# Layer-norm transposes on 64 rows of the array, in two PSUM banks an image, and set-up products in the projection's banks

## The chip, the cores and the metric

The kernel runs on one core of one Trainium2 chip. The metric is the device time of one execution in microseconds; a lower number is better. The core has TensorE (PE, with its weight loads shown apart as PEld), VectorE (DVE), ScalarE (ACT), GpSimd (POOL) and SyncE (SP), 16 DMA engines shared by the queues, and PSUM, which holds what PE writes[...].

## The reference

`x` is float32, 16 images of 192 channels by 64 x 64 pixels. Two layers follow each other. Only the first lines concern the change:

```
h = layernorm over the 192 channels of each pixel (x)
projected, gate = split(h @ in_proj_w.T + b)        # 192 -> 2 x 192 channels
projected = depthwise3x3(projected)
scanned = mix of four directional scans of projected; local = depthwise3x3(projected)
mixed = (scanned + local) * sigmoid(gate)
mixed = gelu(batchnorm over images and pixels (mixed))
x = x + out_proj(mixed)
x = x + fc2(gelu(fc1(layernorm(x))))
# second layer
taps = small network of the mean of x over pixels      # per image and channel
out = masked depthwise3x3(x, taps) + bias
```

## The kernel before

Three stages run one after the other. The first (to about 628 us) does the layer norm and the input projection of all images and stores the result to HBM. The second (to about 1300 us) does the depthwise convolutions, scans, gate and the sums of the batch norm, by groups of 8 channels. The third does the rest by chunks of 512 pixels of an image pair. The change touches only the first.

The instructions of the five engines run in the order in which the program text issues them; semaphores that the framework derives from tiles hold them apart. A tile pool gives a tag so many buffers; a new tile of a tag waits until the readers and writers of the tile that had the buffer are done.

The first stage has 64 steps n (`n_ac`). A step holds 512 pixels of two images: `xa` is [128, 3, 512], where partitions 0 to 63 hold 64 channels of the first image, partitions 64 to 127 those of the second, and the middle index t runs over the three classes of 64 channels. `HALF` names the two partition halves, and `pixels(n, t, g)` is one class of one group g of 128 pixels; a step has AR = 4 groups. Four steps make a block (16 image rows of a pair).

For each step:

- `load_a(n + 3)` issues six loads of 128 KB (L473), three on SP's queue and three on POOL's. `xa` has four buffers, so a load waits until the projection of step n - 1 is done.
- `store_first` (L532) and `store` (L538) issue the stores of the block before, part by part (`PARTS` cuts the channel groups into 1, 7, 7, 5 and 3), on the SP and POOL queues.
- `turn(n + 1)` transposes the next step's pixels on PE into `ps_xt` (L485), so that each pixel has its channels along the free axis: 12 transposes of 128 x 128, for 3 classes and 4 groups. `ps_xt` has one buffer of three banks.
- `project(n)` (L514) multiplies, for each group, the raw pixels by the projection's weights, which already hold the layer norm's scale and have their column means taken away. For each of three classes there are two products, one for each image on its 64 rows of the array, [64 x 128 pixels] by [64 x 384], summed over the classes in PSUM tiles `ps_pj0` and `ps_pj1` of two buffers each. FP32 products appear as two records in the profile, transposes as one.
- `variance(n + 1, g)` on DVE takes the statistics of the next step's group g for both images (`bn_stats` L492, `bn_aggr` L493), issued ahead of the evacuation of group g.
- The evacuation multiplies the projection by 1/deviation and writes it to a staging tile: DVE takes `ps_pj0` (L519), ACT takes `ps_pj1` (L520). Blocks alternate between the staging tiles `stg` and `mid`, so the first evacuation of a block waits for the stores of the block before the last.
- `deviation(n + 1)` takes the square root on ACT (L497) and the reciprocal on DVE (L498).
- `side` adds set-up work to some steps: `diagonals`, `gate_bias`, `decay_rows`, `projection_bias`, `tap_sums`, `columns`, `sums_across`, `conv_bias`, `runs` and others. Those with a product on PE (steps 5 to 8 and 18 to 23, and two before the loop) take a PSUM bank from `bank()`, tag `pb` with one buffer (L268).

PSUM is filled before and after: before, `pb` has one bank, `xt` three and the `pj` tiles four.

The order of PE in step n is: turn(n + 1), projection of groups 0 to 3 of step n, set-up products of step n.

Of the kernel before, what the change touches and what calls it, by code (L numbers as in the profile page):

```python
# [21 lines left out]
F32 = mybir.dt.float32  # L22
# [5 lines left out]
C = 192  # L28
# [3 lines left out]
CH = 512  # L32
# [12 lines left out]
AR = CR // 2  # L45
# [10 lines left out]
def conv_block_kernel(ctx: ExitStack, tc: tile.TileContext, x, prm, w_in, w_out, w_fc1, b_fc1, w_fc2, w1, bn1, w2, out):  # L56
    nc = tc.nc
# [5 lines left out]
    HALF = (slice(0, 64), slice(64, 128))  # L63
# [26 lines left out]
    ident = cp.tile([128, 128], F32, tag="ident", name="ident")  # L90
# [159 lines left out]
    with ExitStack() as stage:  # L250
# [15 lines left out]
        ind = ka.tile([128, 3], F32, tag="ind", name="ind")  # L266

        def bank():  # L268
            return psa.tile([128, CH], F32, tag="pb", name="pb")

        def projection_weights():

            by_group = lambda v: v.rearrange("p (k g c) -> p g k c", k=2, c=GC)
            flat = lambda v: v.rearrange("p g k c -> p (g k c)")
            for t in range(3):
                nc.vector.tensor_scalar_mul(wi[:, t], by_group(w0[:, t]), pt3[:, t, LN1W:LN1W + 1])
            yield
            pc = bank()
            for t in range(3):
                nc.tensor.matmul(pc[:, 0:2 * C], mean_w, flat(wi[lo, t]), start=(t == 0), stop=(t == 2))  # L280
            yield
            for t in range(3):
                nc.vector.tensor_sub(flat(wi[:, t]), flat(wi[:, t]), pc[:, 0:2 * C])
            yield
# [11 lines left out]
        def gate_bias():  # L296
            pb = bank()
            for t in range(3):
                nc.tensor.matmul(pb[:, 0:C], lnb[:, t], w0[lo, t, C:2 * C], start=(t == 0), stop=False)
            for t in range(3):  # L300
                nc.tensor.matmul(pb[:, 64 * t:64 * t + 64], ones[lo], dg[:, t, 0], start=False, stop=(t == 2))
            nc.vector.tensor_copy(bias_g, pb[:, 0:C])
# [7 lines left out]
        def decay_rows():  # L310
            pd = bank()[:, 0:2 * C].rearrange("p (k c) -> p k c", k=2)
            for t in range(3):
                for k in range(2):
                    nc.tensor.matmul(pd[:, k, 64 * t:64 * t + 64], ones[lo], dg[:, t, 1 + k],
                                     start=(t == 0 and k == 0), stop=(t == 2 and k == 1))
            for k in range(2):
                by_half(dec_b[:, k], pd[:, k])
# [140 lines left out]
        psa = stage.enter_context(tc.tile_pool(name="psa", bufs=1, space=PSUM))  # L458
# [18 lines left out]
        def pixels(n, t, g):  # L477
            return ast[n]["xa"][:, t, g * 128:(g + 1) * 128]

        def turn(n):  # L480

            xt = psa.tile([128, 3, AR, 128], F32, tag="xt", name="ps_xt")
            for t in range(3):
                for g in range(AR):
                    nc.tensor.transpose(xt[:, t, g], pixels(n, t, g), ident)  # L485
            ast[n].update(xt=xt, st6=sp.tile([128, AR, 2, 6], F32, tag="st6", name="st6"),
                          mv=sp.tile([128, AR, 2, 2], F32, tag="mva", name="mva"))

        def variance(n, g):
            s = ast[n]  # L490
            for i, q in enumerate(HALF):
                nc.vector.bn_stats(s["st6"][:, g, i], s["xt"][:, :, g, q])  # L492
                nc.vector.bn_aggr(s["mv"][:, g, i], s["st6"][:, g, i])  # L493

        def deviation(n):
# [5 lines left out]
        def project(n, groups, beside_it):  # L501

            blk, part = divmod(n, per)
            if blk not in stag:
                if blk % 2:
                    both_i = mid.rearrange("p (i o j) -> p i o j", i=2, j=BR)
                else:
                    both_i = stg.tile([128, 2, 2 * C, BR], F32, tag="stg", name="stg")
                stag[blk] = [both_i[:, i] for i in range(2)]
            for g in groups:  # L510
                ps = [psa.tile([128, 2 * C], F32, tag=f"pj{i}", name=f"ps_pj{i}", bufs=2) for i in range(2)]
                for t in range(3):
                    for i, q in enumerate(HALF):
                        nc.tensor.matmul(ps[i], pixels(n, t, g)[q], wi[q, t].rearrange("p g k c -> p (g k c)"),  # L514
                                         start=(t == 0), stop=(t == 2))
                for v in beside_it(g) if n + 1 < n_ac else ():
                    variance(n + 1, v)
                j, rs = part * AR + g, ast[n]["rs"]
                nc.vector.tensor_scalar_mul(stag[blk][0][:, :, j], ps[0], rs[:, g, 0:1])  # L519
                nc.scalar.activation(stag[blk][1][:, :, j], ps[1], AF.Copy, scale=rs[:, g, 1:2])  # L520
# [44 lines left out]
        next(steps)  # L565
        next(steps)
        turn(0)
        for g in range(AR):
            variance(0, g)
        deviation(0)  # L570

        for n in range(n_ac):
            if n + 3 < n_ac:
                load_a(n + 3)
            blk, part = divmod(n, per)
            if blk:
                if part == 0:
                    store_first(blk - 1)
                    store(blk - 1, 0, (nc.gpsimd, nc.sync))
                store(blk - 1, part + 1, (nc.gpsimd, nc.sync))  # L580
                if part == per - 1:
                    stag.pop(blk - 1)

            h = AR // 2 if n == 0 else 0
            project(n, range(h), lambda g: ())
            if n + 1 < n_ac:
                turn(n + 1)
            project(n, range(h, AR), lambda g: (g,) if h == 0 else (2 * (g - h), 2 * (g - h) + 1))
            if n + 1 < n_ac:
                deviation(n + 1)  # L590
            for f, args in side.pop(n, ()):
                f(*args)
# [5 lines left out]
    with ExitStack() as stage:  # L598
# [168 lines left out]
        for k in range(-2, n_bp + 1):  # L767
            if 0 <= k + 1 < n_bp:
                tables(k + 1)
            if k >= 1:  # L770
                vertical(k - 1)
                gate(k - 1)
                g, c = divmod(k, hp_)
# [645 lines left out]
```

## Time and profile before

| | |
|---|---|
| median of 3 runs | 3594.07 us (3593.32 to 3596.56) |
| profiled execution | 3596.65 us, span 3594.9 us |
| busy share of the span | PE 99%, PEld 52%, DVE 76%, ACT 51%, POOL 32% |
| first stage, last projection record | 628.0 us |
| `ps_pj` L514, PE | 516.1 us, 3072 records, 488 ns mean |
| `ps_xt` L485, PE | 768 records, 273 ns median |
| `st` L492, DVE | 173.1 us, 512 times, 338 ns mean |
| granted clock of PE | 0.997 of full speed |

A record's length includes its latency, and records overlap: what an engine can do per microsecond is read from the distance between starts, not from the mean length. The DMA share is the mean busy share of the 16 engines; packets of two queues overlap in it, so it can pass 1.

### The profile page before, as it was taken

What the parts mean: (1) busy time and instruction counts of PE and PEld (TensorE: products, weight loads), DVE (VectorE), ACT (ScalarE), POOL (GpSimd) and SP (SyncE); (2) the same over time, 40 slices, a digit from 0 to 9 for tenths busy, and PEclk for the clock granted to TensorE, in tenths of its full rate; (3) what the DMA queues carried; (4) which work ended last, traced back from release to release, by engine and by line L of the source; (5) the groups of instructions that cost most, each with busy time, mean ns of one, the idle gap of its engine ahead of it and who ended that gap; (6) DMA issues with size and microseconds to landing.
All of it is one profiled execution on the core that took longest, in us unless ns stands there. A gap on an engine that the chain in (4) does not pass through costs nothing.

```text
span 3594.9 us, 77663 instructions
## 1 busy us (share of the span) xinstructions
PE 3572.8 (99%) x32658; PEld 1885.2 (52%) x32658; DVE 2748.3 (76%) x4722; ACT 1836.6 (51%) x2067; POOL 1156.2 (32%) x1246
## 2 busy tenths in 40 slices
PE   9999999999999999999999999999999999999998
PEld 6666666555566654445444444445444444444443
DVE  6878777899999985556777777677777767777765
ACT  3443334888888863434444453444445444444533
POOL 3434332111111123433333343433333343333433
PEclk9999999999999999999999999999999999999999
DMA  7898998999999961112222222222222222222213
GB/s 165 240 257 254 258 271 242 301 301 283 281 283 286 281 143 41 45 44 72 60 68 75 65 74 61 79 60 68 73 66 74 61 79 60 69 75 65 74 34 89
DMA packets 288981, 492.19 MB, mean 137 GB/s; under 512 B 24816, under 2 KB 183016, under 8 KB 288632
## 3 DMA queue, kind: packets, MB, share of 16 engines
q1 hardware_dynamic: 246772, 341.85, 35.5%
q0 software_dynamic: 40928, 144.36, 14.1%
q8 instruction: 257, 4.21, 0.5%
q10 hardware_dynamic: 932, 1.03, 0.1%
q14 instruction: 92, 0.75, 0.1%
HBM read 284.95 MB, written 197.92 MB: 134 GB/s over the span
## 4 chain that ended last, share of the span: by engine, by line
PE 90%; DVE 1%; DMA 1%; issue 0%; ACT 0%; ACTq 0%; SPq 0%; POOL 0%; DVEq 0%
PE ps_f L996 28%; PE ps_f L851 18%; PE ps_l L673 11%; PE ps_pj L514 8%; PE ps_d L629 7%; PE ps_s L851 7%; PE ps_o L906 5%; PE ps_o L899 2%; PE ps_xt L485 1%; PE ps_m L935 1%; PE ps_v L935 1%; PE ps_k L851 0%; DMA xa<-in_x_dram 0%; DVE o L65 0%; PE pb_h L141 0%
## 5 line engine op out<-in xcount | busy, mean ns | idle before, releaser
L996 PE MATMUL ps_f<-h,wf 64*64 64x512 f32 x9216 | 1015.0, 591 | 0.0
L998 ACT ACTIVATE gl<-ps_f,bf 128x1024 f32<-128x1024 f32 x384 | 427.9, 1114 | 1082.0 <-PE ps_f L996 1079.7
L996 PEld LDWEIGHTS ps_f<-h,wf 64*64 64x64 f32 x9216 | 346.9, 133 | 598.4 <-issue 574.6
L851 PE MATMUL ps_f<-gl,place 128*64 128x256 f32 (+1 forms) x3072 | 528.7, 486 | 1.1 <-ACT rs L978 1.1
L514 PE MATMUL ps_pj<-wi,xa 64*128 64x384 f32 x3072 | 516.1, 488 | 1.6 <-DVE mid L519 1.0
L514 PEld LDWEIGHTS ps_pj<-wi,xa 64*128 64x128 f32 x3072 | 292.8, 188 | 196.4 <-issue 11.6
L1031 POOL TENSOR_TENSOR gl<-gl 128x512 f32<-128x512 f32 x192 | 308.8, 1635 | 159.1 <-PE ps_f L851 159.1
L851 PEld LDWEIGHTS ps_f<-gl,place 128*64 128x64 f32 x3072 | 225.5, 137 | 217.4 <-issue 145.7
L1021 POOL COPY turn<-o 128x1 f32<-128x1 f32 x84 | 16.4, 195 | 832.8 <-DVE o L65 832.8
L1027 POOL TENSOR_TENSOR t<-gl 128x512 f32<-128x512 f32 x192 | 246.1, 1282 | 89.1 <-ACT gl L998 44.7
L1029 POOL TENSOR_TENSOR t<-gl,t 128x512 f32<-128x512 f32 x192 | 247.1, 1287 | 44.2 <-ACT gl L998 30.7
L473 POOL DMA_DIRECT2D xa<-in_x_dram x192 | 120.4, 635 | 362.5 <-PE ps_pj L514 319.8
L65 DVE SCALAR_TENSOR_TENSOR o<-ximg,taps,o 128x1024 f32<-128x1024 f32 x180 | 231.7, 1288 | 4.9
L664 DVE TENSOR_TENSOR_SCAN v<-tab,q 128x1024 f32<-128x1024 f32 x96 | 218.3, 2274 | 7.8 <-ACT tab L652 7.8
L666 DVE TENSOR_TENSOR_SCAN v<-tab,q 128x1024 f32<-128x1024 f32 x96 | 217.5, 2266 | 0.0
L520 ACT ACTIVATE mid<-ps_pj,rsa 128x384 f32<-128x384 f32 x128 | 120.3, 941 | 184.9 <-PE ps_pj L514 178.6
L520 ACT ACTIVATE stg<-ps_pj,rsa 128x384 f32<-128x384 f32 x128 | 120.3, 941 | 180.6 <-PE ps_pj L514 176.3
L1054 DVE SCALAR_TENSOR_TENSOR ximg<-ps_f,pt,ximg 128x256 f32<-128x256 f32 (+1 forms) x176 | 96.6, 549 | 151.2 <-PE ps_f L851 151.2
L652 ACT ACTIVATE tab<-mask,dec_b 128x1024 f32<-128x1024 f32 x192 | 209.8, 1146 | 0.0
L492 DVE BATCH_NORM_STATS2 st<-ps_xt 128x6 f32<-128x192 f32 x512 | 173.1, 338 | 15.6 <-PE ps_xt L485 14.8
L912 DVE SCALAR_TENSOR_TENSOR ximg<-ps_o,pt,low 128x256 f32<-128x256 f32 x264 | 113.1, 479 | 92.9 <-PE ps_o L906 90.2
L906 PE MATMUL ps_o<-low,wo 128*64 128x256 f32 x1536 | 182.1, 385 | 0.4 <-ACT low L879 0.4
(258 smaller groups left out, 5686.0 us busy)
## 6 DMA issues: line engine op xcount, KB each, us to landing
low<-in_x_dram SPq DMA_DIRECT2D x128, 384.0 KB
out_dram<-o SPq DMA_DIRECT2D x172, 256.0 KB
mid<-pg_d SPq DMA_DIRECT2D x8, 4096.0 KB
low<-mixed_d SPq DMA_DIRECT2D x116, 256.0 KB
low<-pg_d SPq DMA_DIRECT2D x7, 4096.0 KB
pg_o<-pg_d SPq DMA_DIRECT2D x7, 4096.0 KB
xa<-in_x_dram POOLq DMA_DIRECT2D x192, 128.0 KB, 5.6
xa<-in_x_dram SPq DMA_DIRECT2D x192, 128.0 KB
```

What stands on the lines that cost most here:

```text
L65: nc.vector.scalar_tensor_tensor(o, in0, scalar, in1, ALU.mult, ALU.add, **kw)
L514: nc.tensor.matmul(ps[i], pixels(n, t, g)[q], wi[q, t].rearrange("p g k c -> p (g k c)"), start=(t == 0), stop=(t == 2))
L520: nc.scalar.activation(stag[blk][1][:, :, j], ps[1], AF.Copy, scale=rs[:, g, 1:2])
L629: nc.tensor.matmul(dst(ps[o, ih]), mats[g % 2]["dm"][q, di + 1, :, ch], src(s["pg"][q, :, 0, ch]), start=(di == 0), stop=stop)
L673: nc.tensor.matmul(dst(bst[k]["ps"][o, i]), lm_of(g)[q, m, :, c], src(q, ih), start=start, stop=stop)
L851: nc.tensor.matmul(ps[q], w(i), rhs(i), start=start, stop=stop, **kw)
L906: nc.tensor.matmul(ps[wh][q].rearrange("p (r w) -> p r w", w=32), wo[:, 64 * t:64 * t + 64], cols(rows(s["mx"][:, i]))[:, :, wh], start=fi ...
L996: nc.tensor.matmul(pf[o, i], wf1[q, t, m0:m0 + 64], s["h"][q, t], start=(t == 0), stop=(t == 2))
L998: nc.scalar.activation(gl, pf, AF.Gelu, bias=bf1[:, m:m + 1])
L1027: sub(t1[:, m], b12(m), b11(m))
L1029: sub(t2[:, m], b22(m), t1[:, m])
L1031: sub(b12(m), b22(m), b12(m))
```

## The change

`turn` splits each 128 x 128 transpose into two: the first image's 64 channels on rows 0 to 63 of the array and the second image's on rows 64 to 127, each against a 64 x 64 part of the identity. They write two tiles, `xt0` and `xt1`, of two banks each (room for four classes, of which three are used). `variance` reads the image's own tile. That takes four banks in place of three. To make room, `bank()` no longer has a bank of its own: set-up products take one of the two buffers of tag `pj0`. The `pj` tiles are declared a full bank wide and used at 384 of 512 columns.

```diff
         def bank():
-            return psa.tile([128, CH], F32, tag="pb", name="pb")
+            return psa.tile([128, CH], F32, tag="pj0", name="pb", bufs=2)
...
         def turn(n):
 
-            xt = psa.tile([128, 3, AR, 128], F32, tag="xt", name="ps_xt")
+            xt = [psa.tile([128, 4, AR, 64], F32, tag=f"xt{i}", name=f"ps_xt{i}") for i in range(2)]
             for t in range(3):
                 for g in range(AR):
-                    nc.tensor.transpose(xt[:, t, g], pixels(n, t, g), ident)
+                    for i, q in enumerate(HALF):
+                        nc.tensor.transpose(xt[i][:, t, g], pixels(n, t, g)[q], ident[q, q])
...
             for i, q in enumerate(HALF):
-                nc.vector.bn_stats(s["st6"][:, g, i], s["xt"][:, :, g, q])
+                nc.vector.bn_stats(s["st6"][:, g, i], s["xt"][i][:, 0:3, g])
...
-                ps = [psa.tile([128, 2 * C], F32, tag=f"pj{i}", name=f"ps_pj{i}", bufs=2) for i in range(2)]
+                ps = [psa.tile([128, CH], F32, tag=f"pj{i}", name=f"ps_pj{i}", bufs=2)[:, 0:2 * C] for i in range(2)]
```

## The prediction

> **What bounds the kernel now.** I read the page first (busy times, costliest groups), then the table of windows by stage, then the chain of waits inside the first stage, and last the timeline of TensorE (PE) around one image's transposes. The table of windows (columns: window, its length, busy time and instruction count of PE, PE's weight loads, VectorE (DVE), ScalarE, GpSimd; then clock, DMA share, GB/s):
>
> ```profile
> 15.00:100.00 85.00, 84.36 (x547) 54.39 (x547) 65.95 (x216) 30.83 (x41) 23.04 (x40) 0.98 0.64 161
> 100.00:400.00 300.00, 299.69 (x1914) 186.29 (x1914) 239.85 (x754) 121.32 (x158) 117.63 (x199) 1.00 0.90 254
> 400.00:600.00 200.00, 197.84 (x1256) 122.35 (x1254) 148.82 (x442) 79.09 (x105) 78.87 (x138) 1.00 0.95 268
> 600.00:630.00 30.00, 28.97 (x187) 17.68 (x183) 20.65 (x53) 13.40 (x17) 1.71 (x4) 1.00 0.58 185
> 630.00:1300.00 670.00, 670.00 (x7717) 407.55 (x7717) 653.67 (x479) 566.35 (x677) 73.21 (x74) 0.99 1.02 280
> ```
>
> The first stage ends at 628 us. PE is busy throughout it, with DVE at 75 to 80% and the DMA engines at 0.90 to 0.95: PE sets the pace and the DMA stands close behind. The chain of waits within the stage repeats one pair of rows:
>
> ```profile
> 316.10 1.46 PE ps_xt L485 x12
> 317.56 7.94 PE ps_pj L514 x48
> ```
>
> So one step n costs 9.40 us: 12 transposes and 48 records of the projection. The timeline of PE around one set of transposes (start, length, what):
>
> ```profile
> 305.56 1.14 PE L514 MATMUL ps_pj<-wi,xa 64*128 64x384 f32 x6
> 306.63 1.53 PE L485 MATMUL ps_xt<-ident,xa 128*128 128x128 f32 x12
> 308.09 1.24 PE L514 MATMUL ps_pj<-wi,xa 64*128 64x384 f32 x6
> ```
>
> Projection records come in pairs, one on each 64 rows of the array, and pairs start 0.322 us apart (each single start in the trace; in these x6 rows the last pair starts at 306.21). 24 pairs take 7.73 us, so the turn takes 9.40 - 7.73 = 1.67 us. The 12 transposes start 0.109 us apart, 1.31 us; the other 0.36 us is entry and exit: the first is 0.1 us late, the second starts 0.17 instead of 0.11 us after it, and the first projection pair after the turn starts 0.2 us after the last transpose and lasts 587 instead of 482 ns.
>
> **What the Trainium skill says.** "TensorEngine Tiling (Array Packing)", Key Properties: changing the tiling mode drains TensorE, and different tiles load weights and multiply in parallel. The 0.36 us above agrees with a drain on each side of the turn. Restrictions and Gotchas of the same page: row tiles must write different PSUM banks, and transposes of FP32 are excluded with column tiling; row tiling is not in that list. The change keeps to this: the halves write `xt0` and `xt1`. "TensorE: Matmul & The Clock Gate", LDWEIGHTS: a load takes columns / 1.2 ns, whatever the rows. By that a 128-column load takes 107 ns, and halving the rows saves nothing of it. The trace agrees for FP32 products but not for transposes, as the next part shows.
>
> **The change, part by part.**
>
> *The transposes.* 12 of 128x128 go, 24 come with 64 rows, 128 weight columns and 64 moving columns, alternating between row halves. The page has no such row, so I bound it by its neighbours:
>
> ```profile
> L485 PEld LDWEIGHTS ps_xt<-ident,xa x768: 137/140/145, 10.8 to 612.4; 128*128 128x128 f32 x192
> L350 PEld LDWEIGHTS pb<-ident,sv x9: 82/83/83, 200.0 to 239.4; 64*3 64x3 f32 x9
> L325 PEld LDWEIGHTS pb<-pt,place x18: 129/135/136, 95.8 to 96.8; 64*64 64x64 f32 x18
> L314 PEld LDWEIGHTS pb<-wf,ones x12: 187/188/189, 84.8 to 86.2; 64*128 64x128 f32 x12
> 200.34 0.33 PE L350 MATMUL pb<-ident,sv 64*3 64x64 f32 x3
> 85.07 1.45 PE L314 MATMUL pb<-wf,ones 64*128 64x64 f32 x12
> ```
>
> (Loads: min/median/max ns.) Moving side: L350 is a transpose with 64 moving columns and almost no weights; three take 0.33 us and one 0.216, so they start 57 ns apart, half of 109. Weight side: for products 64 more columns cost 188 - 135 = 53 ns, so 128 cost 106, and L314 is held to that: 12 records of 64 moving columns in 1.45 us are 0.11 us apart. For transposes 125 more columns cost only 140 - 83 = 57 ns, so 128 cost 58. A pair side by side therefore takes max(57, 58), about 58 ns, and 12 pairs 0.70 us. Side by side is what L514's pairs show: two starts 7 ns apart, loads of 187 ns for both.
>
> Entry and exit: L350 follows L514 with no gap (last pair 200.01, first transpose 200.34), so a transpose on 64 rows after a projection pair drains nothing. What stays is the release of the old statistics by DVE, which comes 0.07 to 0.17 us before the projection's stream ends, and two semaphore instructions of 51 ns: 0.1 us. The next projection's load of 106 ns behind a 58 ns step adds 0.05. New turn 0.70 + 0.15 = 0.85 us, saving 1.67 - 0.85 = 0.82 us in each of 63 turns of the loop: at most 52 us. Step: 8.58 us.
>
> *Who has to keep up: DVE.* The statistics read as many elements (332 ns median, 512 times), so they cost the same. After the last group DVE evacuates it, takes the reciprocal and does two statistics by 2.7 us after the stream's end, before the next evacuation. That one comes 0.85 + 1.93 + 0.14 = 2.9 us after it, so 0.2 us of the present 1.08 us are left:
>
> ```profile
> 432.53 0.89 DVE L519 TENSOR_SCALAR stg<-ps_pj,rsa 128x384 f32<-128x384 f32 x1 [1.08 <-PE ps_pj L514]
> ```
>
> Steps in which DVE has set-up work of some 2 us (8 to 10 `tap_sums`, 25 to 28 `runs`) lose about 0.6 us of the gain each: 5 us.
>
> *Who has to keep up: DMA.* A step loads 0.79 MB and stores 1.57 MB. At 8.58 us that is 275 GB/s. The ceiling from the table is about 280 (share 1.02 in the second stage); the packets of 100 to 400 us, with the time engines stand empty taken out, give 285. So steps 10 to 40 just fit; some evacuations will wait for stores of the block before (that wait exists now: 3.2 us at step 30). I take 3 us for it. Steps 41 to 59 also carry 4.5 MB of weights and tables: 19 x 2.36 + 4.5 = 49.5 MB at 285 GB/s is 174 us, against 182.5 now (391.2 to 573.7). There the DMA, not PE, is next, and 8.5 us is all that can be had. SP and GpSimd issue the same transfers in the same order; they only wait less for PE.
>
> *Set-up products in `pj0`.* Ten in the loop (steps 5 to 8, 18 to 23), two ahead. Each now takes one of two `pj0` buffers, so it waits for the evacuation two groups back (long done), and the next step's first group waits for that of the last group, 1.04 us after its stream. PE gets there after the turn, 0.85, and the product, 0.17 to 1.45 us; behind it on PE is the projection. I take 0; were the cover gone, 10 x 1 us. It frees nothing: no wait on `pb` holds PE now. The `pj` tiles padded to a bank cost no instruction.
>
> *Sum.* Steps 1 to 9: 9 x 0.82 - 2 = 5. Steps 10 to 40: 31 x 0.82 - 3 - 3 = 19. Steps 41 to 59: 8. Steps 60 to 63: 3. Together 35 us. The second stage starts after the last evacuation and DMA is idle then (2 GB/s in 620 to 630 us), so it moves up whole. The profiled execution took 3596.65 us (span 3594.9), 2.6 above the median of 3594.07, under 0.1%; 3596.65 - 35 = 3561.7, on the median **3559 us**.
>
> **Rivals.**
> (a) DMA and DVE yield more than I think: the full 52 us, **3542**. For it: share 0.90 leaves room until 400 us. Against: 400 to 600 us. Chance 0.10.
> (b) The halves do not overlap, or the DMA holds the whole stage near its present pace. Serial transposes: 24 x 57 = 1.37 + 0.1, a gain of 0.19 x 63 = 12 us, **3582**. For it: no transpose pair on two row halves is in the trace. DMA at 270 GB/s throughout would leave some 15 us, much the same. Chance 0.13.
> (c) Slower: loads bind. If each half's 128 columns load in 107 ns, as products do and the skill's formula says, and the two halves' loads queue for one path, the turn is 24 x 0.107 + 0.15 = 2.7 us, 1.05 more, x 63 = **3660**. It decides from about 65 ns per load in series (24 x 65 = 1.56 us). For it: 24 loads of as many columns replace 12. Against: the 140 ns rows and L514's twin starts. Chance 0.07.
> (d) No effect, the gain eaten by waits for stores or for `pj0`: **3592**. Chance 0.06.
>
> **Numbers.** The worked case has 0.64, its own range 3548 to 3570. With (a) and (b) the range 3542 to 3584 holds 0.87 before errors in these bounds. 0.2%, about what a measurement of this kernel can tell from no change, is 7 us: faster below 3587. Faster 0.85 (worked case, (a), most of (b)), same 0.08, slower 0.07.
>
> **What would show it.** Right: `xt0`/`xt1` transposes starting in pairs some 7 ns apart, pairs 58 ns apart; a first projection pair after the turn at about 482 ns; steps of 8.6 us from 100 to 390 us, 9 to 9.2 us near 400 to 570; DMA share near 1.0 and more waits of evacuations for stores; the first stage ending near 593 us, later stages unchanged in length. Wrong: steps of 9.2 us (pairs in series), above 10 (loads in series), transposes short but steps still 9.3 (DMA), or PE waiting on `pj0` in steps 6 to 9 and 19 to 24.

## The result, and the profile after

| | before | after |
|---|---|---|
| median, run side by side | 3595.32 us | 3560.13 us (3559.31 to 3561.18) |
| ratio, with its interval | | 0.9903 (0.9890 to 0.9916) |
| profiled execution (span) | 3596.65 us (3594.9) | 3559.31 us (3557.5) |
| start of the first stage's last projection record | 628.0 us | 590.7 us |

The kernel became 35 us faster by the medians, 1.0%. The profiled executions differ by 37.3 us, and so do the ends of the first stage (628.0 - 590.7 = 37.3): the whole gain lies in that stage, and the later stages moved up without changing their length. All lines of the kernel after stand one lower in the text: the transposes are L486, the projection L515, DVE's evacuation L520, ACT's L521, and both `xt` tiles appear as `ps_xt`.

The chain of waits inside the stage (start, length, what) has the same pair of rows as before, with a shorter first one:

```profile
323.29 0.75 PE ps_xt L486 x24
324.04 7.80 PE ps_pj L515 x48
```

One step now takes 8.54 us where it took 9.40. The timeline of PE around one set of transposes, and the rows of the transposes' loads and records in the view by tile (duration min/median/max in ns):

```profile
320.53 2.76 PE L515 MATMUL ps_pj<-wi,xa 64*128 64x384 f32 x16
323.11 0.93 PE L486 MATMUL ps_xt<-ident,xa 64*128 64x64 f32 x24
323.86 1.53 PE L515 MATMUL ps_pj<-wi,xa 64*128 64x384 f32 x8
```

```profile
L486 PEld LDWEIGHTS ps_xt<-ident,xa x1536: 134/139/223, 9.7 to 575.4; 64*128 64x128 f32 x192
L486 PE MATMUL ps_xt<-ident,xa x1536: 216/223/367, 9.7 to 575.4; 64*128 64x64 f32 x192
```

From the first transpose to the first projection record there are 0.75 us. By single starts, the two transposes of a pair are 23 ns apart in this turn (10 ns in the median of all turns), and pairs follow each other every 62 ns; 12 x 62 ns is 0.74 us. The first projection pair starts 41 ns after the last transpose, where it took 200 ns before, and lasts 538 ns. The next pair comes 0.379 us later instead of 0.322. The first transpose pair starts 0.32 us after the last projection pair, which is the normal distance between pairs: nothing is lost on the way in. So the turn costs 8.54 - 7.73 = 0.81 us.

The table of windows (columns as in the table of before):

```profile
100.00:400.00 300.00, 295.08 (x2449) 207.03 (x2447) 253.35 (x802) 128.71 (x170) 126.89 (x216) 1.00 0.96 268
400.00:570.00 170.00, 162.62 (x1345) 117.24 (x1343) 128.89 (x392) 69.69 (x94) 69.19 (x120) 0.98 1.01 287
570.00:600.00 30.00, 28.90 (x204) 18.68 (x204) 16.08 (x43) 10.60 (x14) 3.10 (x6) 0.93 0.61 196
600.00:1270.00 670.00, 669.55 (x7706) 381.17 (x7698) 659.79 (x486) 566.05 (x677) 72.70 (x71) 1.00 1.02 279
```

PE now has idle time (5 us from 100 to 400, 7 us from 400 to 570), the DMA share has gone from 0.95 to 1.01 in the second of these, and the second stage reads as before. The gain is not even. I count by intervals, where interval k ends at the start of turn k; the sums of the prediction's steps 10 to 40 and 41 to 59 are these intervals. 0.86 us in each of 63 intervals would be 54 us. Most intervals are at 8.54. Intervals 7 to 10, which hold set-up work too, are long in both kernels (10.98, 10.68, 10.53 and 9.51 before; 9.80, 9.84, 10.11 and 8.90 after). In the following ones the gain fell short most:

| intervals | before, us | after, us | what holds them |
|---|---|---|---|
| 11 to 13 | 9.34, 9.40, 9.40 | 9.25, 9.10, 9.11 | DVE: `tap_sums` |
| 21, 23, 25 | 9.92 each | 9.60, 9.60, 9.64 | PE: products of `sums_across` (L350) and `conv_bias` (L355) |
| 28 to 31 | 9.46, 9.46, 9.98, 9.46 | 9.77, 9.48, 10.08, 9.78 | DVE: `runs` |
| 38, 39 | 9.40, 9.40 | 8.64, 8.92 | DMA: stores |
| 45 to 47 | 10.36, 11.47, 9.40 | 12.01, 11.95, 8.99 | DMA: weights; in 46 TensorE's clock |
| 50, 58 | 10.22, 9.40 | 10.92, 10.86 | DMA: loads and tables |

Two of these rows in the profile. First, PE's timeline in intervals 30 and 31; the brackets are PE's idle time and who ended it. Before the third group's products PE waits about 1 us for DVE to evacuate the first, because DVE was busy with `runs` (2.0 us of fills, copies, a scan and a sum, from 270.69 to 272.72 us):

```profile
269.83 4.09 PE L515 MATMUL ps_pj<-wi,xa 64*128 64x384 f32 x24
275.19 4.14 PE L515 MATMUL ps_pj<-wi,xa 64*128 64x384 f32 x24 [1.27 <-DVE mid L520]
279.17 0.92 PE L486 MATMUL ps_xt<-ident,xa 64*128 64x64 f32 x24
...
284.97 0.59 PE L515 MATMUL ps_pj<-wi,xa 64*128 64x384 f32 x2 [0.96 <-DVE mid L520]
```

Second, the chain of waits at intervals 45 and 46. SP issues a store (L539), which takes 10.77 us while weights come in, and the evacuation that needs the staging tile comes after the store and one more load of weights:

```profile
403.81 0.63 SPq L539
...
404.49 10.77 DMA pg_d<-mid
...
415.27 4.16 DMA w1t<-in_w_dram
```

PE's timeline shows that the two intervals are long for different reasons. In 45 the transposes wait 3.13 us for a load of pixels. In 46 PE is busy nearly throughout, but slow:

```profile
412.46 1.70 PE L486 MATMUL ps_xt<-ident,xa 64*128 64x64 f32 x24 [3.13 <-DMA xa<-in_x_dram]
413.96 6.17 PE L515 MATMUL ps_pj<-wi,xa 64*128 64x384 f32 x24
```

The same instructions take 0.92 and 4.09 us elsewhere. TensorE's granted clock was 0.50 from 411.3 to 418.2 us, after the wait. That is 2.9 of the 3.4 us by which interval 46 exceeds 8.54. The prediction has no term for it.

### The profile page after: what moved, and what is told of

The parts are those of the page before. It is cut to its first block, busy times and chain, and to the rows that moved or that the text cites. A ratio compares the mean times of both kernels' runs of the same rounds, so it can differ in the third digit from the quotient of the medians.

```text
span 3557.5 us, 79074 instructions
## 1 busy us (share of the span) xinstructions
PE 3525.5 (99%) x33426; PEld 1874.6 (53%) x33426; DVE 2741.6 (77%) x4722; ACT 1834.7 (52%) x2067; POOL 1155.7 (32%) x1246
## 4 chain that ended last, share of the span: by engine, by line
PE 89%; DVE 1%; DMA 1%; issue 0%; ACT 0%; SPq 0%; ACTq 0%; POOL 0%; DVEq 0%
PE ps_f L997 28%; PE ps_f L852 19%; PE ps_l L674 11%; PE ps_pj L515 7%; PE ps_d L630 7%; PE ps_s L852 7%; PE ps_o L907 5%; PE ps_o L900 2%; PE ps_m L936 1%; PE ps_v L936 1%; PE ps_xt L486 1%; PE ps_k L852 0%; DMA pg_d<-mid 0%; DMA xa<-in_x_dram 0%; DMA mixed_d<-mid 0%
## 5 line engine op out<-in xcount | busy, mean ns | idle before, releaser
L515 PE MATMUL ps_pj<-wi,xa 64*128 64x384 f32 x3072 | 520.1, 488 | 9.2 <-DVE stg L520 6.2
L515 PEld LDWEIGHTS ps_pj<-wi,xa 64*128 64x128 f32 x3072 | 334.0, 189 | 159.9 <-DVE stg L520 10.5
L521 ACT ACTIVATE mid<-ps_pj,rsa 128x384 f32<-128x384 f32 x128 | 119.5, 937 | 167.0 <-PE ps_pj L515 150.1
L521 ACT ACTIVATE stg<-ps_pj,rsa 128x384 f32<-128x384 f32 x128 | 119.2, 935 | 162.6 <-PE ps_pj L515 144.2
```

## The experiments

My theory: the loads of 128 weight columns set the transposes' pace, and two row halves load side by side, so a pair costs what one did; what leaves the mode of the array also leaves its drains; and the rest of the 54 us is held by DVE in a few intervals and by the DMA from about turn 40 on. The rivals were that the banks made the difference, that the drains and not the pairing made it, and that the stalls belong to something else. Ratios are to the kernel before, on the same chip.

**The banks alone.** The kernel before, with only this part of the change:

```diff
-            return psa.tile([128, CH], F32, tag="pb", name="pb")
+            return psa.tile([128, CH], F32, tag="pj0", name="pb", bufs=2)
...
-                ps = [psa.tile([128, 2 * C], F32, tag=f"pj{i}", name=f"ps_pj{i}", bufs=2) for i in range(2)]
+                ps = [psa.tile([128, CH], F32, tag=f"pj{i}", name=f"ps_pj{i}", bufs=2)[:, 0:2 * C] for i in range(2)]
```

> The kernel before, with only the second part of the change: set-up products take a buffer of tag pj0, and the pj tiles are a bank wide; the transposes stay 128 x 128 in one tile of three banks. My theory: ten set-up products in the loop find their buffer free, so 3595 us, within 2 us of before, steps of 9.40 us. Rival: the buffer shared with the projection costs up to 1 us in each of ten steps (3605), which the shorter transposes of the whole change then cover; or the bank of its own cost something and its removal gives part of the gain (3590).

Measured: 3595.09 us against 3595.97, ratio 0.9998 (0.9989 to 1.0007), and its ordinary intervals stand at 9.40 us. Sharing `pj0` with the set-up products neither costs nor gives anything that can be measured behind a turn of 1.67 us, and the wider `pj` tiles don't either. Behind the short turn of the kernel after, the sharing does cost something; the section on the prediction shows it.

**The same transposes in another order.** From the kernel after: all twelve of the first row half, then all twelve of the second.

```diff
-            for t in range(3):
-                for g in range(AR):
-                    for i, q in enumerate(HALF):
+            for i, q in enumerate(HALF):
+                for t in range(3):
+                    for g in range(AR):
                         nc.tensor.transpose(xt[i][:, t, g], pixels(n, t, g)[q], ident[q, q])
```

> The changed kernel with the 24 transposes in another order: first all 12 of rows 0 to 63, then all 12 of rows 64 to 127. Same instructions, same tiles, no pair of neighbours on different rows. If the gain comes from two row halves working side by side, the turn is 24 x 57 ns = 1.37 us and 0.1 us of entry, 1.47 to 1.5 us against 0.81 in the changed kernel and 1.67 before: steps of 9.2 us and about 3584 us. If the gain comes mainly from the drains of the array that the 128-row transposes need and from earlier entry, the order matters little: steps of 8.6 us, 3560 us.

Measured: 3576.76 us, ratio 0.9946 (0.9932 to 0.9961). Ordinary intervals take 8.90 us, a turn of 1.17. PE's timeline around a turn of this kernel:

```profile
349.30 1.27 PE L486 MATMUL ps_xt<-ident,xa 64*128 64x64 f32 x21
350.36 0.59 PE L515 MATMUL ps_pj<-wi,xa 64*128 64x384 f32 x1
350.41 0.35 PE L486 MATMUL ps_xt<-ident,xa 64*128 64x64 f32 x3
```

A projection record stands between transposes that the program issues ahead of it. By single starts, each half's transposes are 62 ns apart, as in the pairs (which half a record belongs to is inferred from the order of starts), so the pace of one half is the same alone and in company. The first half's twelve run from 349.302 to 349.988, the second half's from 349.804 to 350.541, and the first half's next product starts at 350.357. The halves thus overlap at the borders, which is why I was wrong with 9.2 us: strictly in series the turn would be 24 x 62 ns = 1.49 us, and 0.32 of it went into overlap. The pairing itself is worth 1.17 - 0.81 = 0.36 us a step.

**Four row groups.** Each transpose cut once more, into 32 rows; four parts of one tile, one bank each.

```diff
-            xt = [psa.tile([128, 4, AR, 64], F32, tag=f"xt{i}", name=f"ps_xt{i}") for i in range(2)]
+            xt = psa.tile([128, 4, CH], F32, tag="xq", name="ps_xq")[:, :, 0:3 * AR * 32].rearrange(
+                "p r (t g c) -> p r t g c", t=3, g=AR)
...
-                    for i, q in enumerate(HALF):
-                        nc.tensor.transpose(xt[i][:, t, g], pixels(n, t, g)[q], ident[q, q])
+                    for r in range(4):
+                        q = slice(32 * r, 32 * r + 32)
+                        nc.tensor.transpose(xt[:, r, t, g], pixels(n, t, g)[q], ident[q, q])
...
-                nc.vector.bn_stats(s["st6"][:, g, i], s["xt"][i][:, 0:3, g])
+                nc.vector.bn_stats(s["st6"][:, g, i], s["xt"][:, 2 * i:2 * i + 2, :, g])
```

> The changed kernel with each transpose cut into four of 32 rows, 48 a step, into four banks; the statistics read the same 192 numbers per pixel in as many instructions. A quarter moves 32 columns and still loads 128. If loads set the pace of 58 ns and all row groups load side by side: 12 x 58 ns = 0.70 us, and the change from 64-row to 32-row tiles and back drains the array again as before, 0.36 us: turn 1.06 us, steps of 8.8 us, about 3572 us. If the moving columns set it: 12 x 30 ns + 0.36 = 0.72 us, 3557 us. If loads of different row groups queue for one path: 48 x 58 = 2.8 us + 0.36, steps of 10.9 us, about 3700 us.

Measured: 3568.26 us, ratio 0.9925 (0.9910 to 0.9940). Ordinary intervals take 8.81 us, a turn of 1.08. PE's timeline, and the row of the loads in the view by tile:

```profile
320.06 0.94 PE L488 MATMUL ps_xq<-ident,xa 32*128 32x32 f32 x48
320.93 8.01 PE L517 MATMUL ps_pj<-wi,xa 64*128 64x384 f32 x48
```

```profile
L488 PEld LDWEIGHTS ps_xq<-ident,xa x3072: 132/137/224, 11.4 to 586.6; 32*128 32x128 f32 x192
```

Half the moving columns, half the rows, twice the instructions, and the pace is unchanged: four transposes start within some 15 ns, the next four 62 ns later. So neither the moving columns nor the rows set the pace, and row groups load side by side. What is left is the load of the 128 weight columns, as my theory has it, or a least distance between records of one row group whatever they load: in the kernel before, the transposes of L350 (3 weight columns) start 56 ns apart, and the products of L325 (64 weight columns, 1 moving column) 58 ns. No run varies the weight columns alone, so the pace is measured and its cause is argued. Of the turn, 12 x 61.5 ns = 0.74 us is the transposes and 0.34 is back: the second four start 83 ns after the first, the first projection pair starts 0.15 us after the last transposes and again lasts 587 ns. A first pair of 587 ns also follows a wait of PE between instructions of one mode (at 187.79 us in the kernel after), so this length marks a TensorE that had run empty. The 0.34 us is what the kernel before paid (0.36 us). Both change between the rows of the transposes and the projection's 64; the kernel after does not. This agrees with the Trainium skill, "TensorEngine Tiling (Array Packing)", Key Properties, on both of its points: a change of the tiling mode drains TensorE, and tiles load and multiply in parallel.

**Weights and tables later.** From the kernel after, to see whether the stall of 45 and 46 follows the transfers.

```diff
-            beside(40 + k, load_weights, k)
+            beside(43, load_weights, k)
...
-                beside(45 + 8 * i + 2 * h, load_dm, i, (h,))
-                beside(49 + 8 * i + 2 * h, load_lm, i, (h,))
+                beside(47 + 8 * i, load_dm, i, (h,))
+                beside(51 + 8 * i, load_lm, i, (h,))
```

> The changed kernel with the weights and tables for the second stage loaded at the end of the last step of a block (steps 43, 47, 51, 55, 59), where the stores are smallest, and not at steps 40 to 44 and every second step from 45 to 59. The changed kernel's steps 45 to 47, 50 and 58 are together 12 us longer than 8.54. If the DMA engines withhold this (evacuations waiting for stores that stand behind these loads), the excess falls to some 4 us: 3552 us. If DVE or another engine does, the same steps stay long: 3560 us.

Measured: 3556.48 us, ratio 0.9892 (0.9877 to 0.9907), which the interval does not separate from the kernel after. In the trace the stall moved with the transfers: intervals 45, 46 and 58 are at 8.54, and 47, 48 and 50 take 12.22, 11.61 and 11.26. So the cause is the transfers and not the place; moved within the full stretch, they still cost most of it. I had expected 4 us more than that.

**Weights at the end.** The same loads in steps 60 and 61, where the stage's loads have stopped; `squeeze_scale`, which uses them, follows in step 63.

```diff
-        for k in (0, 1, 3, 4):
-            beside(40 + k, load_weights, k)
+        for k, n in ((4, 60), (3, 60), (0, 61), (1, 61)):
+            beside(n, load_weights, k)
...
-        beside(50, squeeze_scale)
+        beside(63, squeeze_scale)
```

> The changed kernel with the four sets of weights for later stages (1.7 MB) loaded at steps 60 and 61, when the stage's own loads have ended, and not at steps 40 to 44; squeeze_scale moves from step 50 to 63; the tables stay at 45 to 59. In e5_loads_last the long steps moved with the weights from 45 and 46 to 47 and 48 and stayed as long, which fits DMA engines without spare time from 355 us on. If that is so, loads in the end's idle time free 6 to 9 us of the steps near 45 to 50, and nothing is given back: 3552 us. If it is the tables at 45 to 59, or SP's issue alone, the steps stay long: 3560 us; if the second stage waits for these weights, its start is late by what was gained.

Measured: 3551.29 us, ratio 0.9878 (0.9864 to 0.9893). Intervals 45 to 47 are all at 8.54; 50 stays long (9.94), and 58 grows to 13.86. In the profiled execution, the slowest of the four (3554.89 us), the lead over the kernel after is thus 5.2 us at turn 63, less than the 8.8 us between the medians. The stretch from 391 to 434 us in the table of windows, first the kernel after, then this one:

```profile
391.00:434.00 43.00, 39.60 (x313) 33.84 (x311) 29.02 (x90) 15.41 (x22) 13.85 (x24) 0.92 1.01 278
```

```profile
391.00:434.00 43.00, 43.00 (x365) 42.69 (x363) 35.27 (x107) 19.45 (x26) 16.84 (x29) 1.00 0.98 285
```

With the weights gone PE is busy throughout, at a DMA share that is still 0.98: in this stretch the pixels' own traffic just fits at the new pace, and the weights were what did not. Interval 58 holds a wait of 3.39 us and then 3.4 us at a granted clock of 0.50, so that 24 projection records took 5.80 us instead of 4.14.

**`runs` on GpSimd.** Its fills, copies and sum leave DVE; the scan stays there.

```diff
-            nc.vector.memset(imp, 0.0)
-            nc.vector.tensor_copy(imp[:, :, 0:1], gaing[:, c, d:d + 1])
-            nc.vector.memset(dcol[:, :, 0:1], 0.0)
-            nc.vector.tensor_copy(dcol[:, :, 1:HW], decg[:, c, d:d + 1].broadcast_to([NCG, GC // 2, HW - 1]))
+            nc.gpsimd.memset(imp, 0.0)
+            nc.gpsimd.tensor_copy(imp[:, :, 0:1], gaing[:, c, d:d + 1])
+            nc.gpsimd.memset(dcol[:, :, 0:1], 0.0)
+            nc.gpsimd.tensor_copy(dcol[:, :, 1:HW], decg[:, c, d:d + 1].broadcast_to([NCG, GC // 2, HW - 1]))
...
-            nc.vector.tensor_add(vec, vec, run.rearrange("g c m -> g m c"))
+            nc.gpsimd.tensor_add(vec, vec, run.rearrange("g c m -> g m c"))
```

> The changed kernel with the set-up function runs (steps 25 to 28) relieved on DVE: its fills, copies and sum go to POOL, only the scan stays on DVE. In the changed kernel the four steps that begin at 249.8 us take 39.1 us where four of 8.54 would take 34.2. If DVE is what holds them, the excess of 4.9 us falls to about 1: 3556 us. If the DMA or POOL's issue of transfers holds them, it stays or grows, since POOL gets some 4 us more to do in each of these steps: 3560 to 3564 us.

Measured: 3557.18 us, ratio 0.9893 (0.9877 to 0.9910): the median is where it was expected, but the interval alone doesn't separate 3 us. The trace does. In the chain of waits of this kernel the four intervals look like any other; the second of them:

```profile
259.48 0.74 PE ps_xt L486 x22
260.22 7.80 PE ps_pj L515 x48
```

Intervals 28 to 31 sum to 34.46 us instead of 39.11, 4.65 less, so DVE's work in `runs` was what held them. By turn 63 the lead over the kernel after is 2.9 us (571.9 against 574.8): 0.9 went in a later start of turn 1, and some 0.4 each in 32 to 40 and in 41 to 59, where PE's waits for the DMA fell otherwise. (Some of the transposes' records are missing in these rows.)

**Both together** (the last two edits):

> e6_runs_pool and e8_weights_end together. If DVE holds steps 28 to 31 and the DMA holds steps 45 to 50, the gains add: 3548 us, steps of 8.54 us nearly throughout from step 14 on. If both come out of one budget (the DMA engines), the sum is smaller: 3552 us.

Measured: 3547.01 us (3545.54 to 3548.12), ratio 0.9867 (0.9852 to 0.9881). This beats both kernels. Its windows:

```profile
400.00:570.00 170.00, 167.38 (x1398) 129.07 (x1396) 136.12 (x410) 74.07 (x98) 67.40 (x118) 1.00 0.99 284
570.00:600.00 30.00, 28.92 (x256) 23.17 (x256) 13.15 (x18) 14.44 (x22) 4.04 (x7) 0.89 0.96 290
```

The weights fill the stretch from 570 us on (290 GB/s where the kernel after moved 196), and the second stage still starts right behind: from the last projection record to the end it is 2967.5 us here, 2966.8 in the kernel after.

## Why the prediction was right, point by point

*The path.* PE set the pace in nearly all intervals, and the gain per step passed straight to the end. The forecast of 3559 us against 3560 holds by its mechanism; in its parts it was less exact than the total, so that the two lie only 1 us apart is in part luck.

*The transposes.* Forecast 58 ns a pair, measured 62; entry and exit forecast 0.15 us, measured 0.07 (nothing on the way in, 0.06 behind, where 0.05 was forecast). Turn 0.81 for 0.85, step 8.54 for 8.58. Reading the pace from the loads of two transposes with 128 and with 3 weight columns (140 - 83) came within 4 ns; whether the load is its cause stays open, as said at the four row groups. The fallback for it, the Trainium skill's "TensorE: Matmul & The Clock Gate", LDWEIGHTS, with 107 ns for 128 columns, does not hold for these transposes; rival (c) rested on it and on loads in series, and the four row groups refute both. Rival (a) fails on the DVE and DMA intervals, rival (d) on the 8.54 us of the others. Rival (b)'s turn, 24 in series, is excluded by the pairs, and in its own experiment it cost less than its arithmetic; its other half, a DMA held at 270 GB/s, is excluded by the 287 GB/s from 400 to 570 us. Of the 0.86 us saved, the transposes' pace gives 12 x (109 - 62) ns = 0.56 and the drains 0.29; the four row groups put nearly that amount back while keeping the pace.

*By stretches* (us gained to the start of turn 63):

| intervals | forecast | measured |
|---|---|---|
| to 9 | 5 | 6.5 |
| 10 to 40 | 19 | 18.5 |
| 41 to 59 | 8 | 8.1 |
| 60 to 63 | 3 | 3.4 |
| sum | 35 | 36.5 |

*Within 10 to 40* three terms were mis-sized, and with the larger gain per step (0.86 for 0.82) they nearly cancelled. Forecast: 3 us lost to DVE and 3 to waits for stores. Measured, against 0.86 us an interval: 4.2 in 28 to 31 and 1.9 in 11 to 13 to DVE, 1.7 in 21, 23 and 25, and only 0.5 to stores (38 and 39). The first of them is "lose about 0.6 us of the gain each: 5 us" (seven times 0.6 is 4.2). It fits `tap_sums`. With `runs`, DVE had no slack left even before (9.46 against 9.40), so the whole gain was lost there, and another 0.2 us an interval whose cause I have not traced; in "Weights and tables later" and "Weights at the end", which leave `runs` alone, it is 0.1. The second is the waits for stores, 3 us forecast.

*Set-up products in `pj0`*, taken at nothing, are the third. Two kinds of them stand ahead of turns 20 to 25. The kernel after, around turns 20 and 21:

```profile
186.63 0.22 PE L350 MATMUL pb<-ident,sv 64*3 64x64 f32 x1
...
186.83 0.90 DVE L520 TENSOR_SCALAR stg<-ps_pj,rsa 128x384 f32<-128x384 f32 x1 [0.18 <-PE ps_pj L515]
...
187.79 0.62 PEld L515 LDWEIGHTS ps_pj<-wi,xa 64*128 64x128 f32 x6 [0.21 <-DVE stg L520]
...
195.73 0.59 PE L355 MATMUL pb<-wf 3*128 3x192 f32 x2
196.25 0.97 PE L486 MATMUL ps_xt<-ident,xa 64*128 64x64 f32 x24
```

L350 takes one of the two `pj0` buffers, so the next step's first group needs the other, which DVE evacuates until 187.73. PE was through with its last transpose at 187.50 and could have gone on 41 ns after it; it starts at 187.79, 0.25 us late. In a plain turn the first group need not wait: it starts at 323.86 us, before that evacuation is over (324.19). The forecast saw the wait and took it as covered: the evacuation 1.04 us after the stream, against 0.85 for the turn and 0.17 for the product. Measured, PE goes on 1.15 us after the stream and could have at 0.89, because the transposes of the other row half start 13 ns after L350 and run beside it. From the last projection pair ahead of a turn to the first behind it, a plain turn takes 1.07 us; L350 makes it 1.48 (1.88 and 2.04 in the kernel before). So sharing the bank costs nothing with the long turn, as the first experiment shows, and 0.25 us three times with the short one. The 0.25 us are read from the trace; no run gives the kernel after its bank back.

L355 works on 3 rows. It adds 0.67 us to the same distance (1.74 against 1.07), where it added 0.52 before. With four row groups, whose transposes have as small a row tile and start 11 ns after it, it adds 0.37. A change of mode that is now paid for L355 alone fits this (0.30 us less without it, beside the 0.34 of the four row groups), but those transposes also run beside L355, and the two are not separated.

*DMA.* The ceiling was right: from turn 40 to turn 59 the kernel after takes 174.3 us, the forecast was 174, and 400 to 570 us runs at 287 GB/s. The picture of it was not: not every interval stretched to 9 or 9.2 us, but 14 of the 19 kept the 8.54 to 8.55 of PE, and four (45, 46, 50 and 58) carry nearly all of the loss. In 50 and 58 PE waits for an evacuation that waits for a load in flight, in 45 the transposes wait for their pixels, and 46 is long by the halved clock that followed. The forecast had no such term; how much later the stage would have ended at full clock is not shown, because the DMA stayed busy meanwhile (share 1.08 from 411.4 to 418.1 us). Buffers hide the deficit until a block's first evacuation needs its staging tile.

## What to carry to other kernels

When a step gets shorter, add up for every other resource what it must do per step at the new pace, and look for the intervals where it has no slack before the change: those keep their old length, so the gain is counted over the others only. A transfer that nobody needs soon belongs where the DMA is empty; here the intervals in which the weights come in (45 to 47) ran 3 us over their usual length at the old pace and 7 at the new one, and moving the weights brought them back to it. Of the 7 us, 2.9 came through TensorE's clock. A shorter step also takes away the cover of other waits: the shared `pj0` was free behind a turn of 1.67 us and not behind one of 0.81. And instructions between two products of one tiling mode are cheaper in that mode, if they can be split to fit it.

## What was not expected of the hardware

- Transposes of FP32 with 128 weight columns start 62 ns apart with 64 and with 32 rows, alone in their row half or beside others; their loads last 139 and 137 ns (medians).
- Row halves of TensorE are not in step: in the order of two dozens, transposes of the second half started 0.18 us before the last of the first half, and a projection record of one half 0.18 us before the last transposes of the other (350.357 and 350.541).
- A change between transposes of 32 or 128 rows and products of 64 rows cost 0.34 and 0.36 us a turn, both sides together.
- Between turns 40 and 60, eight waits of PE in all these runs lasted 2.2 to 3.6 us. Around the end of seven of them TensorE's granted clock was 0.50 for 3.4 or 6.8 us (after 3.13 us in the kernel after), and not after one of 2.45 us. No wait of up to 2.04 us there was followed by it.
